# Layers 1 and 3 of a sparse four-layer graph kernel: the last chunk of gathered rows expanded by TensorE from rows kept on chip

## The chip, the cores and the metric

The kernel runs on one core of one Trainium2 chip. The metric is device time in microseconds (us) from the first to the last instruction of the slowest core, here the only one. Before the change the median of three runs is 1681.7 us (1679.0 to 1684.24). The core has five engines with queues of their own: PE (TensorE, matrix products), DVE (VectorE), ACT (ScalarE), POOL (GpSimd) and SP (SyncE, which only issues transfers). An engine works through its queue in the order in which the program was built.

## The reference, cut to what matters

Four graph layers run one after the other on x (4096 nodes, 256 features), each on a layer norm with ReLU and each added to x. All use the same adjacency matrix, about 9 neighbours a node.

```python
h = relu(layernorm(x)); x = x + L0(h, adj)   # 8 heads, leaky ReLU of e_l + e_r, a curvature bias, softmax over neighbours
h = relu(layernorm(x)); x = x + L1(h, adj)   # one head:  softmax(leaky(h a1 + h a2)) over neighbours, times h
h = relu(layernorm(x)); x = x + L2(h, adj)   # two softmaxes (e and -e), then a product with wtrans, elu
h = relu(layernorm(x)); x = x + L3(h, adj)   # 4 heads: score = h_n . h_m per head, others score 1.0, softmax, relu
```

A node needs the rows of its neighbours only, so the kernel turns the dense matrix into lists and gathers rows.

## The kernel before

The nodes are cut into 32 tiles of 128 rows. Layer 0 finds, for each tile, the list of the distinct neighbour columns it needs: 9 chunks of 128 slots (`EC = 9`). `nbr[:, t, c]` is the row number for each slot of a chunk. Chunks 0 to 6 (`EARLY = 7`) name rows below 3584 (`NE`), so they can be gathered as soon as the first 28 tiles of a table are written. Chunks 7 and 8 (`LATE = 8`) may name any row; chunk 8 only names rows of the last 512. A layer's table holds one row per node; a gather is one indirect transfer issued by POOL, and fetches 128 rows into one chunk of a tile's buffer `g`. There are six such buffers. Slot 9 (`SELF`) holds the tile's own rows.

```python
    def gather(t, g, table, width, chunks):
        for c in chunks:
            nc.gpsimd.indirect_dma_start(
                out=g[:, c, :width], out_offset=None, in_=table[: NE if c < EARLY else N, :],
                in_offset=bass.IndirectOffsetOnAxis(ap=nbr[:, t, c : c + 1], axis=0),
            )

    # ...
    def gather_early(t, table, width, pool):

        g = pool.tile([P, EC + 1, ROW0], F32, name="g")
        gather(t, g, table, width, range(EARLY))
        return g

    def gather_late(t, g, table, width):
        gather(t, g, table, width, range(EARLY, EC))
        nc.sync.dma_start(g[:, SELF, :width], tile_rows(table, t))

    def summed(o, s, g, width, first=()):

        pairs = list(first) + [(s[:, c, :], g[:, c, :width]) for c in range(EC)]
        for i, (a, b) in enumerate(pairs):
            nc.tensor.matmul(o, lhsT=a, rhs=b, start=(i == 0), stop=(i == len(pairs) - 1))
```

The matrix `st` (a bf16 matrix of 128 rows by 9 x 128 slots) says with ones which row uses which slot. `marked` makes it in layer 1 with ACT and DVE, one buffer `off` between them; it is stored in DRAM (`rows_of`) and loaded again in layers 2 and 3. `bank` is one bank of PSUM.

```python
    def marked(pool, t, st):

        off = pool.tile([P, EC * P], BF16, name="off", bufs=1)
        nc.scalar.activation(off, place, AF.Abs, bias=minus[:, t, 0:1], scale=1.0)
        nc.vector.tensor_scalar(st, off, degree[:, t, 0:1], None, op0=OP.is_lt)
        off = pool.tile([P, (EC - EARLY) * P], BF16, name="off_late", bufs=1)
        nc.scalar.activation(off, place[:, EARLY * P :], AF.Abs, bias=minus[:, t, 1:2], scale=1.0)
        late = st[:, EARLY * P :]
        nc.vector.scalar_tensor_tensor(
```

`run` drives a layer. Each step has a lag: the step with lag k treats tile t in round t + k, and within a round the steps stand in the order of the list. PE's queue is exactly this order; the order of the other engines is set by a scheduler. x stays on chip in `x_all` from layer 1 to the end.

```python
        def run(table, width, steps, first=False):


            of = [{} for _ in range(NT)]

            def loads(t):
                two = t // 2 * 2
                if t == two:
                    of[t]["sts"] = work.tile([P, 2, EC * P], BF16, name="st", bufs=4)
                    if not first:
                        nc.sync.dma_start(of[t]["sts"], rows_of[t // 2])
                st = of[t]["st"] = of[two]["sts"][:, t - two, :]
                if first:
                    marked(work, t, st)
                    if t > two:
                        store(rows_of[t // 2], of[two]["sts"])
                if first and t % XT == 0:
                    nc.sync.dma_start(x_all[:, t : t + XT, :], rows_of_x(x1, t))
                of[t]["x"] = x_all[:, t, :]

            def begin(t):
                of[t]["g"] = gather_early(t, table, width, g_more if t % G1 >= G0 else g_pool)

            def begin_late(t):
                gather_late(t, of[t]["g"], table, width)

            def late_lag(t):

                return (-1, -2, -2, -3, -3)[t] if t < 5 else 2 - G1

            steps = [(-3, loads), (2 - G1, begin), (late_lag, begin_late)] + [
                (lag, lambda t, f=f: f(t, of[t])) for lag, f in steps
            ]
            rounds = {}
            for lag, f in steps:
                for t in range(NT):
                    rounds.setdefault(t + (lag(t) if callable(lag) else lag), []).append((f, t))
            for r in sorted(rounds):
                for f, t in rounds[r]:
                    f(t)


        # give(a, st, own): 9 products of a chunk of st with the own values, then a reduction on DVE
```

Layer 1: `before1` (one round ahead) turns the matrices and forms the row part of the scores, `weigh1` weighs the turned matrices, `attend1` sums, and the finish, `turn2` and `rows2` make the next table's rows.

```python
            def before1(t, of):
                a = of["a"] = work.tile([P, EC + 1], F32, name="a")
                give(a, of["st"], own[0][:, t, :])
                of["s"] = s_chunks(of["st"])

            def give2(t, of):
                give(a2_of[:, t, :], of.pop("st"), own[1][:, t, :])

            def weigh1(t, of):
                s = scores(of["g"], of.pop("a"))
                w = work.tile([P, EC + 1], F32, name="w")
                nc.scalar.activation(w, s, AF.Exp)
                sw = of["sw"] = weights()[:, : (EC + 1) * P].rearrange("p (c r) -> p c r", r=P)
                nc.vector.tensor_mul(
                    sw[:, :EC, :], of.pop("s"), w[:, :EC, None].to_broadcast([P, EC, P])
                )
                nc.vector.tensor_scalar(
                    sw[:, SELF, :], ident, w[:, SELF:], loop[:, t : t + 1], op0=OP.mult, op1=OP.mult
                )

            # ... attend1: summed(o, sw, g, C + 1, [own rows])

            run(table1, ROW1,
                [(3, give2), (0, weigh1), (2, finish1), (1, attend1), (2, turn2), (-1, before1), (2, rows2)],
                first=True)
```

Layer 2 makes the rows of layer 3's table in `rows3`:

```python
            def rows3(t, of):
                pp = times(ps_t, of.pop("hT"), w3_s, C)
                if t % 2 == 0:
                    rows3_of[0] = work.tile([P, 2, C], F32, name="row3")
                row = rows3_of[0][:, t % 2, :]
                nc.vector.scalar_tensor_tensor(
                    row, pp, of.pop("rstd"), b3_s, op0=OP.mult, op1=OP.add
                )
                if t % 2:
                    store_two(table3, t, rows3_of[0])
                nc.vector.tensor_add(all_rows, all_rows, row)
                sq = work.tile([P, D3], F32, name="sq")
                for k in range(K3):
                    nc.scalar.activation(
                        sq, row[:, k * D3 : (k + 1) * D3], AF.Square, accum_out=self3[:, t, k : k + 1]
                    )

```

Layer 3 forms the products `pv` of the matrices with the tile's own rows (fp32, 128 slots x 256), multiplies them with the gathered rows, reduces them by head to scores, and weighs the gathered rows in place before the sum:

```python
            def before3(t, of):
                st = of.pop("st")
                st_f = of["st_f"] = work.tile([P, EC * P], F32, name="st_f")
                nc.scalar.copy(st_f, st)
                s = of["s"] = weights()[:, : EC * P].rearrange("p (c r) -> p c r", r=P)
                nc.scalar.copy(s, s_chunks(st))

            def weigh3(t, of):


                g, st = of["g"][:, :, : C + K3], of.pop("st_f")
                K = EC + 1
                v = work.tile([P, EC, C], F32, name="v", bufs=1)
                s = work.tile([P, K, K3], F32, name="s3")
                for a in range(0, EC, 2):
                    n = min(EC, a + 2) - a
                    pv = bank(ps_v, "pv").rearrange("p (k c) -> p k c", c=C)
                    for k in range(n):
                        nc.tensor.matmul(
                            pv[:, k, :], lhsT=st[:, (a + k) * P : (a + k + 1) * P],
                            rhs=g[:, SELF, :C], start=True, stop=True,
                        )
                    nc.vector.tensor_mul(v[:, a : a + n, :], pv[:, :n, :], g[:, a : a + n, :C])
                nc.vector.tensor_reduce(s[:, :EC, :], heads(v, K3), AX.X, OP.add)
                nc.scalar.copy(s[:, SELF, :], self3[:, t, :])
                nc.vector.scalar_tensor_tensor(s, s, 0.01, s, op0=OP.mult, op1=OP.max)
                nc.scalar.activation(s, s, AF.Exp)
                nc.vector.tensor_scalar(s, s, -math.e, None, op0=OP.add)
                nc.vector.tensor_scalar(
                    s[:, SELF, :], s[:, SELF, :], loop[:, t : t + 1], None, op0=OP.mult
                )
                w = bank(ps_m, "pm")[:, : K * K3].rearrange("p (k h) -> p k h", h=K3)
                nc.scalar.copy(w, s)
                nc.scalar.copy(g[:, :, C:], s)
                gh = heads(g[:, :, :C], K3)
                nc.vector.tensor_mul(gh, gh, w[:, :, :, None].to_broadcast([P, K, K3, D3]))

            def attend3(t, of):
                g = of.pop("g")
                o = of["o"] = bank(ps_o, "o")[:, : C + K3]
                summed(o, of.pop("s"), g, C + K3, [(ident, total_s), (ident, g[:, SELF, : C + K3])])
```

Its steps are `(0, weigh3), (1, attend3), (-1, before3), (2, finish3)`.

Of the kernel before, what the change touches and what calls it, by code (L numbers as in the profile page):

```python
# [20 lines left out]
P = 128  # L21
C = 256
# [689 lines left out]
def gnn_lists(  # L712
# [89 lines left out]
    x1 = dram.tile([N, C], F32, name="x1")  # L802
    rows_of = [dram.tile([P, 2, EC * P], BF16, name=f"rows_of{t}") for t in range(0, NT, 2)]
# [112 lines left out]
    def gather_late(t, g, table, width):  # L916
        gather(t, g, table, width, range(EARLY, EC))
        nc.sync.dma_start(g[:, SELF, :width], tile_rows(table, t))
# [16 lines left out]
    with tc.tile_pool(name="keep", bufs=1) as keep, tc.tile_pool(  # L935
# [570 lines left out]
        def finish0(t):  # L1506
            o, x = of0[t].pop("o"), of0[t].pop("x")
            nc.vector.reciprocal(inv[0][:, t, :], o[:, C:])
            y = work.tile([P, H0, D0], F32, name="y")
            nc.vector.tensor_mul(  # L1510
                y, o[:, :C].rearrange("p (h d) -> p h d", h=H0),
                inv[0][:, t, :, None].to_broadcast([P, H0, D0]),
            )
            nc.vector.tensor_add(x, x, y.rearrange("p h d -> p (h d)"))
            of0[t]["r"], of0[t]["rstd"] = normed(work, x)
            store(tile_rows(x1, t), x)
# [77 lines left out]
    with tc.tile_pool(name="g_more", bufs=G1 - G0) as g_more, tc.tile_pool(  # L1594
# [13 lines left out]
        x_all = kept.tile([P, NT, C], F32, name="x_all")  # L1608
# [11 lines left out]
        def run(table, width, steps, first=False):  # L1620


            of = [{} for _ in range(NT)]

            def loads(t):
                two = t // 2 * 2
                if t == two:
                    of[t]["sts"] = work.tile([P, 2, EC * P], BF16, name="st", bufs=4)
                    if not first:
                        nc.sync.dma_start(of[t]["sts"], rows_of[t // 2])  # L1630
                st = of[t]["st"] = of[two]["sts"][:, t - two, :]
                if first:
                    marked(work, t, st)
                    if t > two:
                        store(rows_of[t // 2], of[two]["sts"])
                if first and t % XT == 0:
                    nc.sync.dma_start(x_all[:, t : t + XT, :], rows_of_x(x1, t))
                of[t]["x"] = x_all[:, t, :]
# [4 lines left out]
            def begin_late(t):  # L1643
                gather_late(t, of[t]["g"], table, width)
# [32 lines left out]
        with tc.tile_pool(name="l1_o", bufs=2, space=PSUM) as ps_o, tc.tile_pool(  # L1677
            name="l1_t", bufs=2, space=PSUM
        ) as ps_t:
# [26 lines left out]
            def finish1(t, of):  # L1706
# [6 lines left out]
                of["r"], of["rstd"] = normed(work, x)  # L1713

# [3 lines left out]
            def rows2(t, of):  # L1718
# [6 lines left out]
                if t % 2:  # L1725
# [4 lines left out]
                table1, ROW1,  # L1730
                [
                    (3, give2), (0, weigh1), (2, finish1), (1, attend1), (2, turn2), (-1, before1),
                    (2, rows2),
                ],
                first=True,
# [15 lines left out]
        with tc.tile_pool(name="l2_o", bufs=1, space=PSUM) as ps_o, tc.tile_pool(  # L1751
# [81 lines left out]
            def finish2(t, of):  # L1833
# [7 lines left out]
                of["r"], of["rstd"] = normed(work, x)  # L1841

            rows3_of = [None]
# [4 lines left out]
            def rows3(t, of):  # L1848
                pp = times(ps_t, of.pop("hT"), w3_s, C)
                if t % 2 == 0:  # L1850
                    rows3_of[0] = work.tile([P, 2, C], F32, name="row3")
                row = rows3_of[0][:, t % 2, :]
# [3 lines left out]
                if t % 2:  # L1856
                    store_two(table3, t, rows3_of[0])
                nc.vector.tensor_add(all_rows, all_rows, row)
# [7 lines left out]
                table2, ROW1,  # L1866
# [12 lines left out]
        with tc.tile_pool(name="l3_o", bufs=2, space=PSUM) as ps_o, tc.tile_pool(  # L1879
            name="l3_v", bufs=3, space=PSUM  # L1880
        ) as ps_v:

            def before3(t, of):
                st = of.pop("st")
                st_f = of["st_f"] = work.tile([P, EC * P], F32, name="st_f")
                nc.scalar.copy(st_f, st)
# [3 lines left out]
            def weigh3(t, of):  # L1890


                g, st = of["g"][:, :, : C + K3], of.pop("st_f")
                K = EC + 1
                v = work.tile([P, EC, C], F32, name="v", bufs=1)
                s = work.tile([P, K, K3], F32, name="s3")
                for a in range(0, EC, 2):
                    n = min(EC, a + 2) - a
                    pv = bank(ps_v, "pv").rearrange("p (k c) -> p k c", c=C)
                    for k in range(n):  # L1900
                        nc.tensor.matmul(  # L1901
                            pv[:, k, :], lhsT=st[:, (a + k) * P : (a + k + 1) * P],
                            rhs=g[:, SELF, :C], start=True, stop=True,
                        )
# [20 lines left out]
            def finish3(t, of):  # L1925
# [10 lines left out]
                if t % XT == XT - 1:  # L1936
                    store(rows_of_x(out, t + 1 - XT), x_all[:, t + 1 - XT : t + 1, :])

            run(
                table3, ROW3,  # L1940
                [(0, weigh3), (1, attend3), (-1, before3), (2, finish3)],
# [104 lines left out]
```

## Time and profile before

| what | number | where it is read |
|---|---|---|
| time, median of three | 1681.7 us | the times |
| span profiled | 1682.5 us, mean granted PE clock 0.892 | the cores |
| gathers | 1152, 0.95 us each on POOL, 1099.7 us in all | the costliest groups |
| first to last gather of layer 1 | 526.94 to 888.97 us | the timeline of POOL |
| of layer 2 | 890.23 to 1250.78 us | the same |
| of layer 3 | 1281.89 to 1644.42 us | the same |
| weighted sums of layer 1 on PE | first 587.48, last 903.46 us | the timeline of PE |
| weighted sums of layer 3 on PE | first 1346.79, last 1660.00 us | the same |
| DMA | 308.56 MB, mean 183 GB/s | the page |

How to read the views. The page gives each engine's busy time and share of the span, and groups of like instructions: line and engine, operation, what is written and read, how many; behind the bar the busy time, the mean ns of one, and the idle time ahead of them with what ended it ("issue" means that the profile shows nothing waited for). The timeline gives start, duration, engine, line, operation, tiles, shape and count, and in brackets the idle time ahead with its releaser; like instructions that follow each other are merged. The table by stretch gives for each piece of the span its length, the busy time of PE, of PE's weight loads, of DVE, ACT and POOL, the granted clock, the DMA share and GB/s. The chain is the work that ended last, followed back from the end. Ends of PE's instructions are modelled, so distances between starts are safer than durations.

### The profile page before, as it was taken

The page shows a single profiled execution, that of the slowest core. Times are in us where ns is not written, and L with a number is a line of the kernel's source. Part 1 is how long each engine was busy: PE and PEld are TensorE (multiplying, and loading weights), DVE is VectorE, ACT ScalarE, POOL GpSimd, SP SyncE. Part 2 cuts the span into 40 slices and gives each one's busy share as a digit, 9 for nine tenths or more (in the row PEclk, how much of TensorE's full clock was granted, in tenths as well). Part 3 has the DMA queues.
Part 4 walks back from the last instruction along what each step waited for, and adds up shares of the span by engine and source line. Part 5 has one row for each costly group of instructions (what it writes and reads, how often), then busy time and mean ns, then how long its engine had stood idle before and what let it go on. Part 6 is the DMA issues. An engine that isn't in the chain of part 4 may idle for free. (4 is left out here: it accounts for less than half of the span.)

```text
span 1682.5 us, 26512 instructions
## 1 busy us (share of the span) xinstructions
PE 1337.2 (79%) x8720; PEld 1077.8 (64%) x8720; DVE 1068.4 (63%) x2955; ACT 666.2 (40%) x1728; POOL 1115.5 (66%) x1210
## 2 busy tenths in 40 slices
PE   4775898889888288767665499999999599999995
PEld 3543666667676177656554387777777377777774
DVE  5756888888865256444442255555555399999995
ACT  3666677776444224323211033433343232223220
POOL 2026665666776777777777777777754777777770
PEclk9977898989898589888787699999999699999998
DMA  8968988996565766655556455555543445555540
GB/s 271 322 238 292 294 304 267 341 306 180 146 171 157 251 160 175 162 158 147 154 152 177 126 152 156 160 145 159 156 136 107 126 142 157 159 160 164 149 125 31
DMA packets 146851, 308.56 MB, mean 183 GB/s; under 512 B 31760, under 2 KB 87312, under 8 KB 146704
## 3 DMA queue, kind: packets, MB, share of 16 engines
q0 software_dynamic: 55296, 153.72, 34.4%
q1 hardware_dynamic: 54914, 115.66, 20.5%
q10 hardware_dynamic: 36494, 37.39, 6.5%
q8 instruction: 71, 1.16, 0.3%
q14 instruction: 76, 0.62, 0.1%
HBM read 271.77 MB, written 34.90 MB: 182 GB/s over the span
## 5 line engine op out<-in xcount | busy, mean ns | idle before, releaser
L905 POOL DMA_INDIRECT g<-table,nbr x1152 | 1099.7, 955 | 440.5 <-issue 338.8
L924 PE MATMUL o<-g,sw 128*128 128x257 f32 (+1 forms) x1216 | 323.2, 427 | 0.0
L924 PEld LDWEIGHTS o<-g,sw 128*128 128x128 f32 x1216 | 259.1, 216 | 46.8
L1796 PE MATMUL o<-g,sw 128*128 128x257 f32 x896 | 202.1, 383 | 35.1 <-DVE sw L1774 34.1
L1796 PEld LDWEIGHTS o<-g,sw 128*128 128x128 f32 x896 | 171.1, 191 | 60.8 <-DVE sw L1774 34.4
L1901 PE MATMUL pv<-g,st_f 128*128 128x256 f32 x576 | 145.0, 397 | 35.6 <-DVE v L1905 35.2
L924 PE MATMUL o<-g,s_f 128*128 128x264 f32 x576 | 153.4, 426 | 0.0
L1901 PEld LDWEIGHTS pv<-g,st_f 128*128 128x128 f32 x576 | 107.1, 195 | 62.0 <-DVE v L1905 48.7
L924 PEld LDWEIGHTS o<-g,s_f 128*128 128x128 f32 x576 | 124.6, 216 | 27.4
L1162 ACT ACTIVATE mask<-adj,minus_half 128x1024 bf16<-128x1024 int32 x112 | 125.4, 1143 | 27.0 <-DMA g<-in_w_t 15.4
L856 ACT COPY hT<-pt 128x256 f32<-128x256 f32 x128 | 47.2, 369 | 169.4 <-PE pt L854 166.1
L1905 DVE TENSOR_TENSOR v<-pv,g 128x512 f32<-128x512 f32 (+1 forms) x160 | 93.3, 630 | 23.3 <-DMA g<-table,nbr 17.2
L854 PE MATMUL pt<-ident,r 128*128 128x128 f32 x256 | 54.6, 298 | 60.6 <-DVE inv L1806 22.3
L863 PE MATMUL pt<-wcat,hT 128*128 128x272 f32 (+2 forms) x384 | 93.3, 361 | 9.6 <-ACT hT L856 6.7
L1181 PE MATMUL kps<-mask,enc 128*128 128x512 bf16 x256 | 84.1, 429 | 15.8 <-ACT mask L1162 11.1
L1499 DVE TENSOR_TENSOR g<-g,pb 128x2560 f32<-128x2560 f32 x32 | 90.1, 2815 | 3.3 <-ACT pb L1496 3.2
L827 ACT ACTIVATE rstd<-mv,eps 128x1 f32<-128x1 f32 (+1 forms) x104 | 30.1, 290 | 154.9 <-DVE mv L834 152.2
L1918 DVE TENSOR_TENSOR g<-g,pm 128x2560 f32<-128x2560 f32 x32 | 89.9, 2810 | 2.0 <-ACT pm L1915 1.8
L854 PEld LDWEIGHTS pt<-ident,r 128*128 128x128 f32 x256 | 33.2, 151 | 90.3 <-issue 38.1
L899 PE MATMUL pm<-own,st 128*128 128x3 bf16 x576 | 24.4, 166 | 81.9 <-DVE own L877 81.1
L887 ACT ACTIVATE off<-place,minus 128x1152 bf16<-128x1152 f16 x64 | 80.1, 1252 | 23.5 <-DVE st L888 22.7
L1605 PE MATMUL s_ps<-ident_b,st 128*128 128x128 bf16 x864 | 65.7, 223 | 27.9 <-DVE sw L1694 27.9
(332 smaller groups left out, 2213.5 us busy)
## 6 DMA issues: line engine op xcount, KB each, us to landing
adj<-in_adj_l SPq DMA_DIRECT2D x128, 512.0 KB
g<-table,nbr POOLq DMA_INDIRECT x1152
st<-rows_of SPq DMA_DIRECT2D x32, 576.0 KB
rows_of<-st ACTq DMA_DIRECT2D x16, 576.0 KB
table<-row ACTq DMA_DIRECT2D x32, 258.0 KB
g<-table SPq DMA_DIRECT2D x64, 129.0 KB
table<-row ACTq DMA_DIRECT2D x32, 135.0 KB
g<-table SPq DMA_DIRECT2D x32, 135.0 KB
```

Source lines behind the costliest of these rows:

```text
L854: nc.tensor.transpose(pt[:, k, :], h[:, k * P : (k + 1) * P], ident)
L863: nc.tensor.matmul(pp, lhsT=hT[:, k, :], rhs=w[:, k, :], start=(k == 0), stop=(k == KC - 1))
L887: nc.scalar.activation(off, place, AF.Abs, bias=minus[:, t, 0:1], scale=1.0)
L905: nc.gpsimd.indirect_dma_start(out=g[:, c, :width], out_offset=None, in_=table[: NE if c < EARLY else N, :], in_offset=bass.IndirectOffset ...
L924: nc.tensor.matmul(o, lhsT=a, rhs=b, start=(i == 0), stop=(i == len(pairs) - 1))
L1162: nc.scalar.activation(m, a, AF.Sign, bias=minus_half, scale=1.0)
L1181: nc.tensor.matmul(kps[h][:KP, :RG], lhsT=enc[0 if on_dve(r, k) else 1][:, at, :], rhs=m[:, i, :], start=False, stop=(at == HB - 1),)
L1499: nc.vector.tensor_mul(gh, gh, w[:, :, :, None].to_broadcast([P, K, H0, D0]))
L1796: nc.tensor.matmul(o, lhsT=sw[:, h, i].rearrange("p s r -> p (s r)"), rhs=g[:, c, : C + 1], start=(i == 0), stop=(i == HC + 1),)
L1901: nc.tensor.matmul(pv[:, k, :], lhsT=st[:, (a + k) * P : (a + k + 1) * P], rhs=g[:, SELF, :C], start=True, stop=True,)
L1905: nc.vector.tensor_mul(v[:, a : a + n, :], pv[:, :n, :], g[:, a : a + n, :C])
L1918: nc.vector.tensor_mul(gh, gh, w[:, :, :, None].to_broadcast([P, K, K3, D3]))
```

## The change

In layers 1 and 3 chunk 8 is no longer gathered. Its rows all lie in the last 512 of the table; these 512 rows are kept on chip, as three bf16 parts that add up to the fp32 row exactly (`late_rows`). For each tile a matrix of ones (`to`, 4 blocks of 128 x 128) says which kept row goes to which slot; it is made in layer 1 with one product (`go_to`) and a comparison, stored behind `st` in `rows_of`, and loaded again in layer 3. TensorE multiplies it with the parts, 4 x 3 products into one bank, and ACT copies the result to the place of chunk 8. This is for taking one of nine gathers per tile away from POOL. The kept rows and their parts need room, so x no longer stays on chip: it is stored after each layer and fetched four tiles at a time. Layer 3's products `pv` take the own rows in the same three parts, stored by layer 2 (`own3`), with the bf16 matrix as it is; its fp32 copy `st_f` goes away. The diff, cut:

```diff
@@ gathers, scratch @@
-    x1 = dram.tile([N, C], F32, name="x1")
-    rows_of = [dram.tile([P, 2, EC * P], BF16, name=f"rows_of{t}") for t in range(0, NT, 2)]
+    xs = [dram.tile([N, C], F32, name=f"x{i}") for i in (1, 2, 3)]
+    LB = (N - NE) // P
+    rows_of = [dram.tile([P, 2, (EC + LB) * P], BF16, ...) ...]
+    own3 = [dram.tile([P, 2, 3, C], BF16, name=f"own3_{t}") for t in range(0, NT, 2)]
-    def gather_late(t, g, table, width):
-        gather(t, g, table, width, range(EARLY, EC))
+    def gather_late(t, g, table, width, chunks=range(EARLY, EC)):
+        gather(t, g, table, width, chunks)
@@ kept rows, expansion @@
-        x_all = kept.tile([P, NT, C], F32, name="x_all")
+        late_rows = kept.tile([P, LB, 3, ROW1], BF16, name="late_rows")
+        col_late = kept.tile([P, NT], F32, name="col_late")
+        late_no = kept.tile([P, LB], F32, name="late_no")
+        def in_parts(parts, row, rest):
+            nc.scalar.copy(parts[0], row)
+            nc.vector.tensor_sub(rest, row, parts[0])
+            nc.scalar.copy(parts[1], rest)
+            nc.vector.tensor_sub(parts[2], rest, parts[1])
+        def keep_late(table, width):        # two blocks at a time: load, in_parts
+            ...
+        def go_to(t, to):
+            pm = bank(ps_e, "pe")[:, :P]
+            nc.tensor.matmul(
+                pm, lhsT=col_late[:, t : t + 1].to_broadcast([P, P]), rhs=ident, start=True, stop=True
+            )
+            nc.vector.tensor_tensor(
+                to.rearrange("p (b e) -> p b e", b=LB), pm[:, None, :].to_broadcast([P, LB, P]),
+                late_no[:, :, None].to_broadcast([P, LB, P]), op=OP.is_equal,
+            )
+        def expanded(t, of, width, pool, name):
+            to = of.pop("to")
+            ps = bank(pool, name)[:, :width]
+            for b in range(LB):
+                for i in range(3):
+                    nc.tensor.matmul(
+                        ps, lhsT=to[:, b * P : (b + 1) * P], rhs=late_rows[:, b, i, :width], ...
+                    )
+            nc.scalar.copy(of["g"][:, LATE, :width], ps)
@@ run @@
                 if first:
                     marked(work, t, st)
+                    go_to(t, of[t]["to"])
-                of[t]["x"] = x_all[:, t, :]
+                four = t // XT * XT
+                if t == four:
+                    of[t]["xs"] = fetch(work, rows_of_x(x_of, t), [P, XT, C], "x")
+                of[t]["x"] = of[four]["xs"][:, t - four, :]
-                gather_late(t, of[t]["g"], table, width)
+                gather_late(t, of[t]["g"], table, width, range(EARLY, LATE if expand else EC))
@@ layer 1 (ps_e: one bank) @@
+            late_i = kept.tile([P, LB], I32, name="late_i")
+            nc.gpsimd.iota(late_i, [[P, LB]], base=NE, channel_multiplier=1)
+            nc.vector.tensor_copy(late_no, late_i)
+            nc.vector.tensor_copy(col_late, nbr[:, :, LATE])
+            keep_late(table1, ROW1)
-                    (2, rows2),
+                    (2, rows2), (-1, expand1),
@@ layer 2, rows3 @@
+                in_parts([parts[:, i, :] for i in range(3)], row, rest)
+                if t % 2:
+                    store(own3[t // 2], rows3_of[1])
@@ layer 3 (expand3 takes a bank of ps_v, three banks, shared with pv) @@
+            keep_late(table3, C)
-                st_f = of["st_f"] = work.tile([P, EC * P], F32, name="st_f")
-                nc.scalar.copy(st_f, st)
-                        nc.tensor.matmul(
-                            pv[:, k, :], lhsT=st[:, (a + k) * P : (a + k + 1) * P],
-                            rhs=g[:, SELF, :C], start=True, stop=True,
-                        )
+                        for i in range(3):
+                            nc.tensor.matmul(
+                                pv[:, k, :], lhsT=st[:, (a + k) * P : (a + k + 1) * P],
+                                rhs=parts[:, i, :], start=(i == 0), stop=(i == 2),
+                            )
-                [(0, weigh3), (1, attend3), (-1, before3), (2, finish3)],
+                [(0, weigh3), (1, attend3), (-1, before3), (2, finish3), (-1, expand3), (-2, own_parts)],
```

## The prediction

> **What bounds the kernel now.** I read the page from the top: busy shares first, then the costliest group, then one table by stretch, and last the chain inside each layer. The shares and the group:
>
> ```profile
> PE 1337.2 (79%) x8720; PEld 1077.8 (64%) x8720; DVE 1068.4 (63%) x2955; ACT 666.2 (40%) x1728; POOL 1115.5 (66%) x1210
> L905 POOL DMA_INDIRECT g<-table,nbr x1152 | 1099.7, 955 | 440.5 <-issue 338.8
> ```
>
> No engine is full over the span, so the shares decide nothing. The gather line does: 1152 gathers (9 a tile, 32 tiles, 4 layers) of 0.95 us, with idle time "issue" before nearly each. In the timeline of POOL the starts are 1.25 us apart (580.23, 581.48, 582.73). A POOL that shows 76% is thus full. At 9 gathers it needs 11.25 us a tile, at 8 it needs 10.0. The starts in order give: layer 1 from 526.94 to 888.97, layer 2 from 890.23 to 1250.78, layer 3 from 1281.89 to 1644.42, with one large hole, at the turn from layer 2 to 3:
>
> ```profile
> 1250.78 0.94 POOL L905 DMA_INDIRECT g<-table,nbr  x1 [0.30 <-issue]
> 1281.89 0.94 POOL L905 DMA_INDIRECT g<-table,nbr  x1 [30.17 <-PE o L1796]
> ```
>
> By this alone 64 gathers fewer would be worth 64 x 1.25 = 80 us. The table by stretch (sum of busy us on PE, PEld, DVE, ACT, POOL; clock; DMA) says why I do not believe it:
>
> ```profile
> 587.00:680.00 93.00, 78.66 (x576) 67.32 (x573) 55.72 (x191) 32.45 (x94) 70.46 (x75) 0.88 0.63 165
> 680.00:890.00 210.00, 147.53 (x1002) 125.01 (x998) 95.89 (x329) 55.79 (x159) 159.35 (x167) 0.80 0.59 158
> 950.00:1251.00 301.00, 277.33 (x1471) 231.56 (x1470) 158.24 (x482) 113.32 (x468) 227.83 (x241) 0.99 0.56 156
> 1346.00:1660.00 314.00, 291.41 (x1493) 242.18 (x1493) 292.14 (x400) 88.73 (x182) 224.88 (x237) 1.00 0.48 144
> ```
>
> In layer 3 DVE and PE are both 93% busy: 292.14/31 = 9.42 and 291.41/31 = 9.40 us a tile. POOL runs 42 early gathers ahead before the first tile can be worked on (layer 1: from 526.94, first weighted sum at 587.48; layer 3: from 1281.89, first at 1346.79), so **compute may be slower per tile than POOL's average and still end with it**. Layer 3's last weighted sum starts at 1660.00; (1660.0 - 1346.8)/31 = 10.10 us a tile. In layer 1 the sums start from 587.48 to 903.46: 10.19 a tile. Only what lowers these two paces is gained.
>
> The pace of layer 3 while nothing is starved, from the chain that ended last:
>
> ```profile
> 1371.51 2.80 DVE g L1918
> 1374.31 0.61 DVE v L1905
> 1374.97 1.56 PE pv L1901 x6
> 1376.53 4.84 PE o L924 x22
> 1381.39 0.03 DVE inv L1927
> ```
>
> It is a ring: sum `o`, reciprocal, weighting of g, first v, the last three fp32 products pv, next `o`: 9.98 us. Layer 1 at the same point is a PE queue with one hole, the wait on `own`:
>
> ```profile
> 608.35 0.38 PE L854 MATMUL pt<-ident,r 128*128 128x128 f32 x2
> 608.57 0.37 PE L899 MATMUL pm<-own,st 128*128 128x3 bf16 x9
> 608.79 0.66 PE L1605 MATMUL s_ps<-ident_b,st 128*128 128x128 bf16 x9
> 609.29 0.56 PE L863 MATMUL pt<-wcat,hT 128*128 128x2 f32 x4
> 611.05 0.39 PE L899 MATMUL pm<-own,st 128*128 128x3 bf16 x9 [1.20 <-DVE own L877]
> 611.30 4.58 PE L924 MATMUL o<-g,sw 128*128 128x257 f32 x20
> ```
>
> One round is 7.4 us with `o` in 4.58; others have `o` in 6.27, and eleven rounds from 587.48 to 679.96 average 8.41.
>
> **What the Trainium skill says.** "DMA: Bandwidth & Descriptors", SWDGE vs HWDGE vs iDMA: a DMA issued from GpSimd has its descriptors computed by software there. The trace agrees: 0.95 us of POOL for a gather of 128 rows. "FP8 and Floating Point Precision", TensorE Precision Notes: true fp32 takes four passes. The trace agrees: 11 fp32 products of 260 columns in 4.84 us are 0.44 each; nine bf16 transposes of 128 columns take 0.66, a single one 0.22, so they follow at (0.66 - 0.22)/8 = 0.055, and 256 columns are estimated at 0.11. "TensorE: Matmul & The Clock Gate", Part 1: the HAM clock gate, gives half clock after an idle window; the granted 0.80 to 0.88 of layer 1 and the 6.27 beside 4.58 fit. The same page, Architectural detail: the array is 16× 32×32, has DVE and ACT as strict FIFO; in this trace every DVE wait holds what stands behind it, and that matters below.
>
> **The change, part by part.** (1) Layers 1 and 3 lose 32 gathers each: POOL's floor falls from 11.25 to 10.0 us a tile.
>
> (2) Layer 1, PE: 12 bf16 products of 258 columns, 12 x 0.11 = 1.32, and one fp32 go_to of 128 columns, about 0.22. In the built program both stand between L863 and the products on `own`, that is, in the 1.2 us hole. But go_to shares its one PSUM bank with the expansion and waits for ACT's copy (0.37 as the hT copy, 0.65 with latencies). Round at full clock: 0.22 + 0.24 + 0.50 + 0.56 + 1.32 + 0.65 + 0.22 + 0.25 + 4.4 = 8.4, against 7.4. The denser PE should lose less clock, so I add 0.7 rather than 1.0 for it: 9.1 a tile, below POOL's 10.0. DVE gets an is_equal of 128x512 (about 0.68, as v), ACT a copy; both have room (DVE 55.72/93).
>
> (3) Layer 1, start. In the new order the row numbers `late_no` come from an iota that stands on POOL behind the 42 early gathers, so they come at 580.23 at the earliest; DVE's queue holds everything behind it, the marks of the first tiles included, which before ran at 551 to 562. Then five marks in turn between ACT and DVE at about 2.0 (1.25 + 0.1 + 0.57 + 0.1), the splits of the kept rows (four ACT copies of 0.5, four subtractions of 0.65) and the expansion come before the first score: from 581.5 I count to about 595.7 against 584.47, first sum at about 600 against 587.48, ended at 606. Six late gathers, not twelve, are done by 588.7; POOL then stands until 606 for the buffer. From there 26 tiles x 10.02 = 260.5: layer 1's gathers end at 866.5 against 890.2. Layer 2 also needs table rows of tile 27: 606 + 28 x 9.1 = 861, plus 5 for turning, storing and landing: 866. Both bounds agree: **21 to 24 saved, I take 21.**
>
> (4) Layer 2 keeps 9 gathers and its 31 us hole. Two ACT copies (0.37) and two DVE subtractions (0.42) a tile go into a stage where DVE idles 3.3 us a tile for a gather; PE gets nothing. x now goes through DRAM: some 29 MB more (x stored and loaded twice 16.8, the own parts 12.6, the wider matrices 8.4, gathers 8.6 less), beside a DMA share of 0.56. I charge 1 us.
>
> (5) Layer 3, PE: 27 bf16 products x 0.11 = 2.97 for 9 fp32 x 0.44 = 3.96; the expansion adds 1.32; together +0.3 a tile, but the piece within the ring falls from 1.56 to about 1.0. ACT loses the 1.15 us copy st_f and gains one of 0.37. The ring becomes about 9.5; DVE's 9.42 with its short waits on ACT (0.3 + 0.26) is then the floor at some 9.7, and I expect 9.85: 31 x (10.10 - 9.85) = 8. The first tile starts 1.25 earlier. Splitting the last rows (about 4 us) hides under the 42 early gathers. **8 saved.**
>
> Sum: 1681.7 - 21 + 1 - 8 = 1654 (rounded).
>
> **Rivals.** *POOL bounds throughout*: the full spacing of 1.25 speaks for it, the 93% of DVE and PE in layer 3 and the head start against. It gives 1681.7 - 80 = 1602. *Layer 1 turns PE-bound*: if the clock falls to half in each round or go_to waits long for ACT, a round is 10 us or more and layer 1 gives nothing: 606 + 280 + 5 = 891. Then 1675. *Layer 3 slows*: the expansion shares three PSUM banks with pv; a wait there of 0.4 a tile costs 31 x 0.4 = 12, so 1666 with layer 1's gain kept. *No late start*: if DVE is not held behind the iota, layer 1 gives up to 35 and the total is near 1640.
>
> **Range and chances.** Layer 1 between 3 and 33 saved and layer 3 between +5 and -13, seldom both at one end: 1640 to 1677. Faster by 2% needs 33.6 us, more than the 28 of the sum: 0.27. Slower by 2% needs both rivals at once: 0.03.
>
> **What would show it.** 1088 gathers still at 1.25; a hole on POOL near 589 to 606; first sum of layer 1 near 600; sums of layer 1 about 9.1 apart; layer 2's first gather near 867 and its length unchanged at 362 plus a hole near 31; sums of layer 3 about 9.85 apart with DVE the busiest. The prediction is wrong if layer 1's rounds exceed 9.8, if layer 2 changes length, or if layer 3 follows POOL at 10.0 rather than its ring.

## The result, and the profile after

The changed kernel takes **1661.5 us** (median of four runs, 1657.7 to 1663.3) against 1681.1 of the kernel before: a ratio of 0.988, with a 95% interval of 0.9855 to 0.9902, 19.6 us less. Predicted were 1654 us in a range of 1640 to 1677. The total lay within the range, and that is in part luck: the terms for layer 2 and layer 3 came out 3.5 and 6.8 us worse, both in the same direction, and 6.0 us behind the last sum, which the prediction did not have, made up for more than half of it.

The page after, its engine line and the gather group (us and share; then busy us, mean ns, idle before):

```profile
PE 1365.9 (82%) x9840; PEld 1110.0 (67%) x9840; DVE 1112.2 (67%) x3061; ACT 673.6 (41%) x1832; POOL 1059.7 (64%) x1147
L910 POOL DMA_INDIRECT g<-table,nbr x1088 | 1044.0, 960 | 450.6 <-issue 323.2
```

There are 64 gathers fewer at about the same price (960 ns each, 955 before). What they bought is read from POOL's timeline after (start, duration, what was issued, idle time before it and who ended it):

```profile
585.79 0.95 POOL L910 DMA_INDIRECT g<-table,nbr  x1 [0.30 <-issue]
604.84 0.94 POOL L910 DMA_INDIRECT g<-table,nbr  x1 [18.10 <-PE pm L904]
...
1231.64 0.95 POOL L910 DMA_INDIRECT g<-table,nbr  x1 [0.30 <-issue]
1265.93 0.94 POOL L910 DMA_INDIRECT g<-table,nbr  x1 [33.34 <-DVE inv L1872]
```

The first pair is the predicted hole at the start of layer 1; the second is the turn from layer 2 to 3. Set beside the same starts of the kernel before, they give the account by layer. "Sums" are the weighted sums `o`; their pace is taken between the first and the last of a layer's 32 reciprocals of `o`, divided by 31.

| stretch | before | after | predicted saving | measured saving |
|---|---|---|---|---|
| first gather of layer 1 to first of layer 2 | 526.94 to 890.23 | 526.63 to 869.77 | 21 | 20.2 |
| to the first gather of layer 3 | 1281.89 | 1265.93 | -1 | -4.5 |
| to the start of the last tile's products `o` | 1660.00 | 1642.86 | 8 | 1.2 |
| pace of layer 1, us a tile | 10.12 | 9.04 | | |
| pace of layer 3, us a tile | 10.16 | 10.12 | | |

With 0.3 us ahead of layer 1 that is 17.1 us up to the last sum. The two profiled spans differ by 23.1 (1682.5 and 1659.4): the rest, 6.0, lies behind the last transfer that the program issues, from which it is 13.4 us to the end before and 7.4 after; the change touches nothing there. The profiled run of the kernel before was also the longest of its four, so part of it is spread; the medians differ by 19.6.

### The profile page after: what moved, and what is told of

Same layout as the page of the kernel before. It is cut to its first block, busy times and chain, and to the rows that moved or that the text cites. A ratio compares the mean times of both kernels' runs of the same rounds, so it can differ in the third digit from the quotient of the medians.

```text
span 1659.4 us, 29109 instructions
## 1 busy us (share of the span) xinstructions
PE 1365.9 (82%) x9840; PEld 1110.0 (67%) x9840; DVE 1112.2 (67%) x3061; ACT 673.6 (41%) x1832; POOL 1059.7 (64%) x1147
## 3 DMA queue, kind: packets, MB, share of 16 engines
q1 hardware_dynamic: 68802, 135.59, 24.4%
## 4 chain that ended last, share of the span: by engine, by line
PE 32%; POOL 17%; DVE 16%; issue 12%; DMA 11%; ACT 4%; ACTq 0%; DVEq 0%; POOLq 0%
POOL g L910 17%; PE o L929 13%; DMA g<-table,nbr 10%; PE o L1862 5%; DVE v L1989 2%; DVE s L1990 2%; PE pt L1895 2%; PE pv L1985 2%; PE pt L868 2%; PE pt L859 1%; PE kps L1186 1%; PE s_ps L1610 1%; DVE g L1504 1%; ACT off L892 1%; DVE stats L838 1%
## 5 line engine op out<-in xcount | busy, mean ns | idle before, releaser
L910 POOL DMA_INDIRECT g<-table,nbr x1088 | 1044.0, 960 | 450.6 <-issue 323.2
L929 PE MATMUL o<-g,sw 128*128 128x257 f32 (+1 forms) x1216 | 283.4, 388 | 0.0
L929 PEld LDWEIGHTS o<-g,sw 128*128 128x128 f32 x1216 | 231.3, 192 | 35.2
L1862 PEld LDWEIGHTS o<-g,sw 128*128 128x128 f32 x896 | 170.9, 191 | 63.4 <-DVE sw L1840 37.0
L1985 PE MATMUL pv<-parts,st 128*128 128x256 bf16 x864 | 106.0, 277 | 16.6 <-DVE v L1989 16.2
L1985 PEld LDWEIGHTS <-st 128*128 128x128 bf16 x864 | 85.7, 99 | 32.2 <-issue 20.8
L1993 ACT ACTIVATE s<-s 128x40 f32<-128x40 f32 x32 | 7.6, 236 | 227.6 <-DVE s L1992 227.6
L1661 PEld LDWEIGHTS <-st 128*128 128x128 bf16 x768 | 77.4, 105 | 22.7 <-issue 11.5
```

What stands on the lines that cost most here:

```text
L910: nc.gpsimd.indirect_dma_start(out=g[:, c, :width], out_offset=None, in_=table[: NE if c < EARLY else N, :], in_offset=bass.IndirectOffset ...
L1862: nc.tensor.matmul(o, lhsT=sw[:, h, i].rearrange("p s r -> p (s r)"), rhs=g[:, c, : C + 1], start=(i == 0), stop=(i == HC + 1),)
L1985: nc.tensor.matmul(pv[:, k, :], lhsT=st[:, (a + k) * P : (a + k + 1) * P], rhs=parts[:, i, :], start=(i == 0), stop=(i == 2),)
```

## The experiments

The experiments ran on chips on which the kernel before itself takes 2227 to 2274 us, so each ratio below is to the kernel before, measured beside it on the same chip, and both kernels of the case were run there as well. "On record" means the runs and profiles of the section above. What differs there can be seen. In layer 3 ACT copies the turned matrices as soon as PE has finished the nine transposes `s_ps`. In the profile of the changed kernel on record the copy starts at most 0.04 us after the later of PE's recorded end and ACT's own last instruction, in all 32 tiles, 28 of them with a gather under way between the first transpose and the copy. In the run of the changed kernel here that holds for the 13 tiles without a gather. Of the 19 with one, 12 start 0.8 to 2.4 us late (median 2.3); in the other 7 ACT itself was busy until 2.4 to 4.0 us after PE's end. In the kernel before, run here, the delay beside gathers reaches 14.3 us. Hand-overs from DVE to ACT and from ACT to DVE in the same layer stay at 0.03 us (medians of 76 and 53), with a gather or without. **What PE finishes reaches ACT and DVE late while POOL issues gathers; what ACT and DVE finish does not.** Whether PE itself ends late or its signal travels late the trace can't say: the Trainium skill, "Perfetto Trace Analysis", Tensor Engine Instruction, notes that the end of a product in a profile is an estimate from its size, not an observation. Stretches without gathers show no such delay (at most 0.5 us in e8), and there the same program runs at the same pace in both places (shown below for the last rounds of layer 3). So I read two things from these runs: differences in ratio, which hold for these conditions, and the rounds without gathers, which hold for both.

All runs, with paces as above and the turn as the time from the last gather of layer 2 to the first of layer 3:

| run | ratio to before (95%) | layer 1 | layer 2 | turn | layer 3 |
|---|---|---|---|---|---|
| e8, kernel before | one run | 13.37 | 14.02 | 38.6 | 13.79 |
| e6, changed kernel | 1.0056 (1.0027 to 1.0086) | 14.84 | 14.48 | 41.7 | 12.51 |
| e1, iota early | 1.0038 (1.0013 to 1.0062) | 13.89 | 14.27 | 44.1 | 12.47 |
| e5, the same again | 1.0029 (1.0005 to 1.0053) | 14.70 | 14.15 | 41.6 | 12.47 |
| e2, layer 1 only | 1.0104 (1.0023 to 1.0184) | 14.17 | 13.97 | 39.7 | 13.91 |
| e3, layer 3 only | 0.9917 (0.9888 to 0.9947) | 13.36 | 14.25 | 43.0 | 12.42 |
| e4, moves only | 0.9964 (0.9935 to 0.9992) | 13.36 | 14.27 | 43.1 | 12.88 |
| e7, three repairs | 1.0127 (1.0094 to 1.016) | 14.08 | 14.24 | 43.3 | 12.97 |
| e9, one part in layer 1 | 0.9778 (0.9743 to 0.9813) | 12.31 | 14.33 | 41.6 | 12.42 |
| e10, own bank for go_to | 0.9782 (0.9745 to 0.982) | 12.71 | 13.95 | 42.6 | 12.44 |
| e11, one part in layer 3 | 1.037 (1.0307 to 1.0432) | 14.51 | 14.22 | 41.3 | 14.89 |
| e12, own bank, iota early | 0.9763 (0.9718 to 0.9808) | 12.34 | 14.24 | 43.6 | 12.53 |

Code that is the same repeats to 0.1 us a tile in layer 3 (12.42 to 12.53 in seven runs) but only to 1 us in the expanded layer 1 (13.89 to 14.84 in six). Smaller differences in layer 1 are read only where all runs agree on the sign.

### The two kernels themselves

> The kernel before itself, for its trace under the conditions of the experiments (2240 to 2270 us). From the runs so far, layer 1 should stand at about 13.4 us a tile as in the runs without expansion, layer 2 at about 14.0 as in the run without the own parts, layer 3 at about 13.9 as in the run with its fp32 products. If one of the three is lower, moving x through DRAM costs something in that layer as well.

> The changed kernel itself beside the kernel before, under the conditions of the experiments. Where the kernel before takes 1681 us: 1661, as on record. Where it takes 2240 us, as in the runs so far: the two kernels with the early iota and without it should then differ by what the late start is worth; if the iota is the late start, this one is some 10 us slower than the 2246 of the early iota; if splitting and expanding set the start, the two agree.

Layers 1 and 2 of the kernel before came as expected (13.37 and 14.02), layer 3 at 13.79. Moving x through DRAM therefore costs nothing visible in layer 1 (13.36 in the moves-only run). The changed kernel, a gain of 1.2% on record, is here **0.6% slower**: it loses (14.84 - 13.37) x 31 = 46 us in layer 1 and wins (13.79 - 12.51) x 31 = 40 in layer 3. The 46 is a high value, because the kernel before took 2274 us beside this run and 2249 in its own; the same layer 1 took 13.89 to 14.70 in the other runs. The ratio with the early iota (1.0029 to 1.0038) overlaps with that without it, so "the two agree" applies, as far as some 6 us can be told apart.

### One half of the change alone

```diff
 e2  layer 3:  [(0, weigh3), (1, attend3), (-1, before3), (2, finish3)]   # 9 gathers, fp32 pv, no own parts
 e3  layer 1:  -  (-1, expand1) ... expand=True     # 9 gathers; go_to and the iota stay
 e4  both:     -  expand1, expand3, go_to, iota     # x through DRAM and the bf16 pv stay
```

> Layer 1 expands as in the changed kernel, layer 3 is again that of the kernel before (9 gathers, fp32 products pv, no parts made in layer 2); x still goes through DRAM. If layer 3 was on DVE's ring before and stays on it, its expansion bought nothing (10.2 us a tile both ways) and layer 2 loses the work for the parts: 1657 to 1662. Rival: the expansion of layer 3 gave the 8 us of the prediction: about 1669.

> Layer 3 expands, layer 1 gathers all 9 chunks; the one-hot matrices and so the late iota are still made in layer 1. If layer 1 gave the whole gain and its late start costs 12 us where POOL is the bound, this is slower than the kernel before: 1681 + 12 (start) + 4 (layer 2) - 1 = about 1696. If the late start is hidden: about 1684. Rival (layer 3 gives 8): 1677 or, with the late start, 1688.

> No expansion in either layer and no one-hot matrices (so no iota); x through DRAM, and the own parts with bf16 products pv in layer 3 stay. The cost of the moves alone: in the changed kernel layer 2 and its turn took 4.4 us longer (1.3 in the gathers, 3.1 in the hole), so about 1685. If the moves are hidden: 1681. If the bf16 pv shortens the ring of layer 3 as predicted: about 1677.

None of the three came where I expected it, because I had written for the pace on record. By layer they are plain. The expansion costs layer 1 some 0.5 to 1.5 us a tile here: 13.89 to 14.84 in the six runs with it, 13.36 or 13.37 in the three without. The bf16 products, which also spare ACT the copy `st_f`, give layer 3 0.9 (13.79 to 12.88), the expansion there about another 0.5 (to 12.42). The two runs in which layer 2 makes no own parts (e8, e2) turn in 38.6 and 39.7 us; the ten that make them need 41.3 to 44.1. The means are 39.2 and 42.6, 3.4 apart; on record the turn grew by 3.2. **So the longer turn is the work of the parts (made in layer 2 and stored), some 3 us, and x through DRAM is at most 1 of it.**

### The late start of layer 1

```diff
+    nc.gpsimd.iota(late_i, [[P, LB]], base=NE, channel_multiplier=1)   # beside the other constants, before layer 0
-            nc.gpsimd.iota(late_i, ...)                                  # behind the early gathers
```

> Only the row numbers late_no move: the iota and its cast run at the start of the kernel instead of behind the 42 early gathers of layer 1. If the late start of layer 1 is that iota (DVE idle 24.42 us before the cast in the changed kernel), the marks run again at 551 to 570, the first sum of layer 1 comes near 588 to 590 instead of 600, POOL's hole of 18 us shrinks to about 6 to 8, and since a PE round of 8.4 us is shorter than POOL's 10.0 the gain is passed on: about 1650 us, 10 to 12 below the changed kernel. Rival: the splitting of the kept rows and the expansion themselves set the start; then the first sum stays near 598 to 600 and the time near 1661.

> The kernel with the early iota once more, because its first run was on a chip on which the kernel before itself takes 2240 us[...]. Where the kernel before takes 1681 us: about 1650 if the iota is the late start (first sum of layer 1 at 588 to 590, POOL's hole of 18 us down to 6 to 8); near 1661, with the first sum still at 598 to 600, if splitting the kept rows and expanding set the start.

The first sum of layer 1 came 83.7 and 83.1 us after its first gather, against 82.8 with the late iota. Nothing was gained, but this does not clear the iota for the case on record: here the last tiles of layer 0 still occupy DVE 56 us after the first gather, and DVE idled only 3.4 us for the iota, against 24.4 on record. What the runs do show is the weight of the rest. The first score comes 68.1 us after the first gather without one-hot matrices (e4), 68.6 with them and the late iota (e3), and 72.4 to 75.3 in the runs that also split the rows and expand. The first sum is later than that of the kernel before by 11.9 us here (82.8 against 70.9) and by 12.9 on record (73.4 against 60.5). This speaks for splitting and expanding as the larger part on record too, but doesn't show it, since PE's results come late here.

### What the expansion costs layer 1

e9 leaves out the second and third part of the kept rows in layer 1, so its rows lose bits; e10 computes the same as the changed kernel.

```diff
 e9 (shortened)
-                for i in range(3):      # expanded, layer 1
+                for i in range(1):
 e10
-            pm = bank(ps_e, "pe")[:, :P]     # go_to: the expansion's only bank
+            pm = bank(ps_t, "pt")[:, :P]     # a bank of the transposes
```

> The changed kernel, but the expansion of layer 1 leaves out the second and third part: 4 products instead of 12 a tile, with the same waits, copies and comparisons (its rows lose bits). Layer 1 stands at 14.7 us a tile with the expansion here and at 13.4 without. If PE's work sets that, 8 x 0.11 = 0.9 us a tile go (28 us, layer 1 at 13.8). If the two further hand-overs from PE (expansion to ACT, go_to to DVE) set it, the layer stays at 14.4 to 14.8.

> The changed kernel with one edit: go_to takes its PSUM bank from the pool of the transposes instead of sharing the expansion's single bank, so it no longer waits for ACT's copy of the expansion (0.46 to 0.77 us of PE in each round of layer 1 in the changed kernel's profile). If that wait is what the expansion costs layer 1: 0.5 to 0.8 us a tile less, 16 to 25 us in all. If the hand-overs as such or POOL set the layer: within 8 us of the changed kernel.

Both beat their expectations. The own bank takes away 1.8 us a tile (14.51 in e11, which ran on the same chip and has the changed layer 1, to 12.71; 1.2 to 2.1 against all six runs of that layer), and one part 2.2, where 0.9 of work was removed. With its own bank layer 1 is also below the 13.36 of the runs without expansion. The wait that e10 removes is seen in the views of PE's waits (us in all, times, longest): of the changed kernel here, from 890 to 1350 us, and then on record, from 600 to 885 us:

```profile
PE pe L1647 <- issue: 106.4, 19, 6.7
PE pe L1647 <- ACT g L1665: 27.8, 9, 5.3
```

```profile
PE pe L1647 <- ACT g L1665: 15.1, 28, 0.8
```

Over 28 tiles that is (106.4 + 27.8)/28 = 4.8 us of PE a tile here and 0.54 on record. In e10 PE never waits before go_to, and its waits in all fall from 5.6 to 3.9 us a tile: part of the time went to other waits. In e9 the wait before go_to is (42.8 + 9.2)/27 = 1.9 us a tile (both from 870 us on, 27 tiles). One instance here, in the timeline of the changed kernel, and then the same two groups in PE's timeline of e10:

```profile
1107.20 1.50 PE L1661 MATMUL pe<-late_rows,st 128*128 128x258 bf16 x12
...
1114.96 0.38 ACT L1665 COPY g<-pe 128x258 f32<-128x258 f32 x1 [5.32 <-DMA g<-table,nbr]
...
1115.39 0.80 PE L1647 MATMUL pe<-ident,col_late 128*128 128x128 f32 x2 [6.69 <-issue]
```

```profile
1046.78 1.50 PE L1661 MATMUL pe<-late_rows,st 128*128 128x258 bf16 x12
1048.12 0.38 PE L1647 MATMUL pt<-ident,col_late 128*128 128x128 f32 x2
```

The bracket of ACT's copy names a gather, but its last wait is for PE: the trace has PE's semaphore at 1114.94. The expansion was over on PE's record at 1108.7, ACT began to empty its bank at 1114.96, and only then could go_to and everything behind it in PE's queue go on, the sum `o` included. With a bank of its own go_to follows without a gap. The Trainium skill says the same in general: "Perfetto Trace Analysis", Matmuls, advises that independent groups rotate through PSUM banks so that ACT or DVE can empty one during the next. The two runs agree with it, and measure it: the shared bank cost some 2 us a tile where what PE finishes arrives late. That one part does as much fits the wait of go_to, which falls there from 4.8 to 1.9 us a tile; why ACT's copy comes so much earlier was not taken apart.

### What sets the pace of layer 3

e11 uses only the first part of the own rows in `pv`, so its scores lose bits; e7 computes the same as the changed kernel.

```diff
 e11
-                        for i in range(3): matmul(pv, st, parts[:, i, :])
+                        matmul(pv, st, parts[:, 0, :])
 e7  (also: iota early, x fetched at lag 0)
-                nc.vector.tensor_mul(y, o[:, :C], inv[3] broadcast)
+                for k in range(K3):
+                    nc.scalar.activation(y[:, k, :], o[:, k * D3 : (k + 1) * D3], AF.Copy, scale=inv[3][:, t, k : k + 1])
```

> The changed kernel, but the products pv of layer 3 use only the first of the three parts: 9 bf16 products instead of 27 a tile (the scores lose bits), 18 x 0.11 = 2.0 us of PE less, nothing else moved. If PE sets the pace of layer 3 (9.60 us of products a tile against 10.1 in the changed kernel's profile), up to 1 to 2 us a tile go, 30 to 60 us. If DVE's ring sets it (weighting, v, sum over columns, score and their waits), layer 3 moves by less than 0.4 us a tile, under 12 us.

> Three separate repairs on the changed kernel, each in a stage of its own, so that the trace tells them apart: the iota of the row numbers at the start of the kernel (layer 1), x fetched three tiles later (turn from layer 2 to 3), and the product y of layer 3 moved from DVE to four ACT copies with a scale (0.42 us of DVE a tile less). Where the kernel before takes 1681 us: first sum of layer 1 near 590 instead of 600 (10 saved) if the iota holds the start, else unchanged; hole at the turn 32 instead of 34 if the fetch of x stands before the last store of the table; sums of layer 3 about 9.8 apart instead of 10.2 (10 to 12 saved) if DVE's ring sets the pace, unchanged if PE (9.60 of products a tile) does. All three: about 1640; none: 1661. Where the kernel before takes 2240 to 2270 us: the ratio to it falls from 1.006 to about 0.995 if DVE's ring sets layer 3 there too, and stays at 1.003 to 1.006 if PE's late results do.

The whole layer became slower in both, against every expectation: 14.89 and 12.97 us a tile against 12.42 to 12.53. The rounds of e11 alternate between about 10 and 21 us. A long one, in the timeline of all engines:

```profile
2007.87 1.49 PE L1661 MATMUL pv<-late_rows,st 128*128 128x256 bf16 x12
...
2019.52 0.95 POOL L910 DMA_INDIRECT g<-table,nbr  x1 [0.30 <-issue]
2021.76 0.37 ACT L1665 COPY g<-pv 128x256 f32<-128x256 f32 x1 [9.92 <-remote]
```

The expansion is finished at 2009.4 by PE's record; ACT's copy of it starts at 2021.76, just after the last gather of a run of gathers (2019.52 to 2020.47). A round that is shorter on paper can so meet a whole run of gathers and wait for its end. Its length here says nothing on PE or DVE.

The last rounds do, since no gather is left. Here the order of DVE's queue matters. Before and after the change every fourth round is a long one, in which the scheduler put the finish of a tile ahead of the next weighting of `g`. In e11 every second round is so, in e7 none: both edits moved DVE's order as well. So I take whole periods, from one weighting on DVE to another: four rounds of the kernel before on record (gathers still run there), four of the changed kernel on record, two of e11, four of e7. In the table by stretch (us, PE, PEld, DVE, ACT, POOL; clock; DMA):

```profile
1616.40:1657.06 40.66, 38.14 (x196) 31.73 (x193) 37.78 (x54) 9.60 (x22) 21.96 (x24) 1.00 0.34 93
```

```profile
1599.42:1639.94 40.52, 38.95 (x276) 33.30 (x273) 37.62 (x53) 8.46 (x24) 0.49 (x1) 1.00 0.06 20
```

```profile
2262.64:2282.98 20.34, 16.23 (x107) 13.23 (x105) 18.78 (x27) 4.24 (x13) 0.00 (x0) 1.00 0.08 27
```

```profile
2195.61:2234.98 39.37, 38.87 (x277) 33.24 (x273) 36.57 (x49) 12.21 (x40) 0.14 (x1) 1.00 0.06 19
```

| us a round | length | PE busy | DVE busy | DVE idle |
|---|---|---|---|---|
| before | 10.17 | 9.54 | 9.45 | 0.72 |
| changed | 10.13 | 9.74 | 9.41 | 0.73 |
| e11, 18 products fewer | 10.17 | 8.12 | 9.39 | 0.78 |
| e7, `y` off DVE | 9.84 | 9.72 | 9.14 | 0.70 |

The change left the round alone. With 1.6 us less of PE it is **not shorter**; with 0.27 less of DVE it is **0.29 shorter**. DVE's idle time stays at 0.7 to 0.8 in all four, whatever the order of its queue, and of 2.5 us of waits in the four rounds of the changed kernel only 0.70 are for PE. Every experiment with its layer 3 repeats these four rounds (9.79, 11.24, 9.38 and 10.11) within 0.03, so they carry over. In rounds without gathers DVE's queue sets the pace of layer 3, and PE's products do not.

### The version that the runs point to

> The version that the runs point to: the changed kernel with go_to in a bank of the transposes (0.978 of the kernel before) and the iota at the start. Here layer 0's last tiles end at about the time at which the late iota runs, so the iota alone gave nothing in two runs: 0.975 to 0.981 of the kernel before, layer 1 at 12.7 us a tile, first sum of layer 1 at 83 us after its first gather. If the iota holds the start of layer 1 here once the bank no longer does, the first sum comes at 76 or earlier and the ratio falls to 0.972 or below.

The two edits together give 0.976 of the kernel before, and beat both kernels here. The interval overlaps with that of the own bank alone, and the first sum came 79.4 us after the first gather (82.0 with the own bank alone), neither 83 nor 76, so a share of the iota in the time is not shown. A gain under the conditions on record is not shown either: go_to waits 0.54 us a tile there, and POOL's 10.0 bounds the later part of the layer.

## Why the prediction was right or wrong, step by step

**(1) POOL's floor** was right: 1088 gathers, still 1.25 us apart.

**(2) Layer 1, PE's round.** The sum of 8.4 at full clock was right, and the 0.7 added for the clock was wrong. PE's timeline after:

```profile
646.67 1.50 PE L1661 MATMUL pe<-late_rows,st 128*128 128x258 bf16 x12
648.85 0.49 PE L1647 MATMUL pe<-ident,col_late 128*128 128x128 f32 x2 [0.67 <-ACT g L1665]
...
649.40 4.58 PE L929 MATMUL o<-g,sw 128*128 128x257 f32 x20
```

The wait of go_to for ACT, put at 0.65, is 0.67 in this round and 0.54 in the mean, and of the first 18 rounds all but one take 8.3 to 8.6. The table by stretch, of after and then of before (us, PE, PEld, DVE, ACT, POOL; clock; DMA), shows why no clock was lost: the filled hole keeps PE at 93% and its clock at 1.00, where 74% had 0.85. (Elsewhere the two go together as well: 92% with 0.99 in layer 2 of the kernel before, 73% with 0.84 in layer 1 of e10.)

```profile
605.00:760.00 155.00, 144.68 (x1233) 125.13 (x1231) 105.97 (x342) 63.60 (x180) 118.13 (x122) 1.00 0.73 211
```

```profile
605.00:760.00 155.00, 115.44 (x834) 98.56 (x832) 82.49 (x284) 51.42 (x141) 117.23 (x125) 0.85 0.62 164
```

It changed nothing in the total, because from the 19th round on the sums wait for POOL. That was the step's claim: below POOL's 10.0. The 9.04 a tile in the table of the result, so near to the 9.1 predicted, is luck: it is the mean of rounds of 8.4 and of rounds that wait for POOL.

**(3) The start of layer 1** came as worked out: the cast of the row numbers at 579.02 (580.23 predicted), the first score at 591.62 (595.7), the first sum at 600.07 (600), its end at 604.6 (606), POOL's hole from 585.79 to 604.84 (588.7 to 606). From there 26 tiles at 10.02 give 865.3; the last gather of the layer stands at 868.52. The share of the iota in it is argued, from the idle time of DVE before the cast, and not shown:

```profile
579.02 0.17 DVE L1739 CAST late_no<-late_i 128x4 f32<-128x4 int32 x1 [24.42 <-POOL late_i L1738]
```

**(4) Layer 2** was a term mis-sized: 1 charged, 4.5 measured. The gathers of the layer take 361.87 us instead of 360.55, and the turn 34.3 instead of 31.1. I had looked at DVE's idle time while gathers bound the layer, and forgot that in the turn nothing is gathered. There three rounds of compute stand on the path, and each has two more DVE operations and two more ACT copies in it. The runs put some 3 us of the turn on the parts; that three rounds stand on the path is argued from the lags. Fetching x later (e7) left the turn at 43.3.

**(5) Layer 3** is the step that failed: 8 us predicted, 1.2 measured. It put the ring at about 9.5 and DVE's floor at 9.7, and expected 9.85; measured are 10.12 against 10.16. The piece of PE in the ring did get shorter. But DVE was already the closer limit, and its floor was mis-sized. Its work was right, 9.42 foreseen and 9.41 measured. The waits of 0.3 + 0.26 on top make 9.98 and not 9.7, a slip in the sum; measured are 0.73 of idle time a round, which is 10.13 with the work. A long round in DVE's timeline after, one of four:

```profile
1537.53 0.18 DVE L2011 RECIPROCAL inv<-o 128x4 f32<-128x4 f32 x1 [0.70 <-PE o L929]
...
1539.32 2.82 DVE L2002 TENSOR_TENSOR g<-g,pm 128x2560 f32<-128x2560 f32 x1 [0.26 <-ACT pm L1999]
```

The finish of a tile comes into DVE's queue ahead of the weighting of the next; it waits 0.70 for the sum, then runs its three operations (with the reciprocal), and the weighting follows 1.8 us later. The kernel before has such rounds as well: there and after they are 11.05 and 11.23 us from sum to sum. e11 and e7 show the rest: less PE does not help, less DVE does, by about as much as is taken away.

**The rivals.** "POOL bounds throughout" fell. "Layer 1 turns PE-bound, because go_to waits long for ACT" did not happen on record and is what happens under the conditions of the experiments, with 13.9 to 14.8 us a tile. "Layer 3 slows by waits for banks" did not happen.

**Left open:** why PE's results arrive late beside gathers on the chips of the experiments, the share of the iota on record, and the 6.0 us behind the last sum.

## What to carry to other kernels

Before an engine's work is cut, ask which engine's ring the stage stands on, and test it in rounds where nothing else is under way: 1.6 us less of PE a tile gave nothing there, 0.27 less of DVE gave 0.29. Take whole periods when rounds differ, and look whether the edit moved an engine's order too. Charge new work to the turns between stages as well, where the idle time of the stage does not exist. And give a short product that opens a round its own PSUM bank, not that of a result that another engine has yet to empty.

## What was not expected of the hardware

What PE hands to ACT or DVE can come late while GpSimd issues gathers: from the transposes to ACT's copy 2.3 us in the changed kernel here (median of 12 tiles), up to 10.1 in e11 and up to 14.3 in the kernel before, against 0.04 on record, with the recorded durations on POOL and DVE unchanged (a gather 0.95, a weighting of 128x2560 2.82). What DVE and ACT hand to each other beside the same gathers stayed at 0.03. Under these conditions the ratio of one and the same change went from 0.988 to 1.006. And a PE that is 93% instead of 74% busy was granted the full clock instead of 0.85, so the added products cost less than their own time: some 2 us of them a round left the early rounds of layer 1 at 8.4 us (8.41 before).
